# Loading weights from another queue, starting two groups side by side, and splitting a deferred product in the last group

## Chip, cores and metric

One core of one Trainium2 chip. All times are device microseconds of that core. The kernel before takes 3486.24 us (median of 3 runs, 3485.54 to 3486.57). Engine names: PE is TensorE, DVE is VectorE, ACT is ScalarE, POOL is GpSimd, SP is SyncE.

## The reference, cut to what matters

Two graph layers, one after the other, on 64 graphs of 256 nodes and 256 features, all in 32-bit floats. The adjacency matrices hold 0 and 1.

```python
x    # (64, 256, 256) float32
adj  # (64, 256, 256) int32, 0 or 1

def gat(h, adj, W, a):                       # twice, W1/a1 and W2/a2
    Wh = h @ W
    e  = leaky_relu(Wh @ a[:F] + swap(Wh @ a[F:]), 0.2)
    return softmax(where(adj > 0, e, -9e15), axis=1) @ Wh

# layer 0
h = layernorm(x + gat(gat(x)), g_ln1, b_ln1)
x = layernorm(h + relu(h @ w_ff1 + b_ff1) @ w_ff2 + b_ff2, g_ln2, b_ln2)
# layer 1: 8 heads of 32; one value matrix per kind of edge (adj == r)
attn = softmax(q @ k.T / sqrt(32))
out  = sum over r of (attn * (adj == r)) @ (x @ Wv[r] + bv[r])
x = layernorm(x + out @ Wo + bo, g1, beta1)
out = layernorm(x + gelu(x @ W1 + b1) @ W2 + b2, g2, beta2)
```

## The kernel before

It takes the graphs in 32 groups of two. A "turn" interleaves the second layer of group `y_`, the feed-forward of the first layer of group `x_ = y_ + 1`, and the graph attention of group `z = y_ + 2`. The order of TensorE's products is the program's order (`manual_schedule`). The parts that matter here, with cuts marked `# ...`:

```python
def load(u):
    xs = io.tile([P, T, F], F32, tag="xs", name=f"xs{u}")          # 2 buffers
    nc.sync.dma_start(xs, x[G * u:G * (u + 1)]...)
    af = io.tile([P, T, N], F32, tag="af", name=f"af{u}", bufs=1)  # 1 buffer
    nc.gpsimd.dma_start(af, adj[G * u:G * (u + 1)]...)
loaded = {0: load(0)}
# ...
def weight(w, name):                       # column() and row() likewise
    t = const.tile([P, w.shape[0] // P, w.shape[1]], F32, name=name)
    nc.scalar.dma_start(t, w.rearrange("(c p) f -> p c f", p=P))
# ... combined graph weights gwe, then some 30 loads on the scalar queue
nc.vector.tensor_tensor(wv[:, :, 1, :], wv[:, :, 1, :], wv[:, :, 0, :], ALU.subtract)
nc.vector.tensor_tensor(rbv[:, F:], rbv[:, F:], rbv[:, :F], ALU.subtract)
# ...
nc.gpsimd.tensor_add(rb1, rb1, rbf2)
nc.gpsimd.tensor_add(rb2, rb2, rbo)
nc.gpsimd.tensor_add(rb3, rb3, rbt2)

def projected(u, hT):                      # xpp, copied out by ACT into xp
    # ...
        nc.scalar.copy(xp[:, t, :], ps[:, :WX])

def normed(u, l, y):
    for t in range(T):
        nc.vector.bn_stats(st[:, t, :], y[:, t, :])
        nc.vector.bn_aggr(mv[:, t, :], st[:, t, :])
    nc.vector.tensor_scalar(ve, mv[:, :, 1], EPS, None, op0=ALU.add)
    nc.gpsimd.tensor_tensor(rs, ve, mhalf, ALU.pow)
    # ...
    for t in range(T):
        nc.vector.tensor_scalar(y[:, t, :], y[:, t, :], mv[:, t, 0:1], rs[:, t:t + 1],
                                op0=ALU.subtract, op1=ALU.mult)

def affine(u, l, xn, g, b):
    r = work.tile([P, T, F], F32, tag="res", name=f"res{u}_{l}", bufs=3)
    nc.gpsimd.tensor_mul(r, xn, g[:, None, :].to_broadcast([P, T, F]))
    nc.gpsimd.tensor_add(r, r, b[:, None, :].to_broadcast([P, T, F]))

def second_sums(x_):                       # ygp: second attention, residual, norm
    # ...
    d["y"] = normed(x_, 0, y)
    d["res"] = affine(x_, 0, d["y"], rg1, rb1)

def turn(y_, x_, z):
    if z + 1 < NG:
        g[z + 1]["xs"], g[z + 1]["af"] = load(z + 1)
    if have(y_): hT = to_features(Y["y"], f"h2T{y_}", lg2, lb2)
    if have(x_): second_sums(x_)
    if have(y_): q, k_ = queries_keys(y_, hT)
    # ... interleaved work of y_, x_ and z
    if have(y_):
        yf = hidden_out(y_, 1, h1, w2, res)          # the last product of a group
        yn = normed(y_, 3, yf)
        res = affine(y_, 3, yn, rg4, rb4)
        nc.sync.dma_start(out[G * y_:G * (y_ + 1)]..., res)

with tc.manual_schedule(engines={mybir.EngineType.PE}):
    for u in range(-2, NG):
        turn(u, u + 1, u + 2)
```

Names of products in the profile: `xpp` projection, `rows` transposed scores, `hpp` first attention sums, `ygp` second attention sums, `h1p` and `yfp` the two feed-forward products, `h1T`, `h2T`, `h3T` transposed and scaled activations, `qp`, `kp`, `vp` queries, keys, values. A number after a name is the group.

## Time and profile before

| | before |
|---|---|
| median of 3 runs | 3486.24 us |
| span of the profiled run | 3486.0 us |
| PE busy | 97% |
| one steady turn (from qp of group 1 to qp of group 2) | 105.79 us |
| fill: start of qp of group 0 | 128.11 us |
| drain: from the end of the last full turn's h1p (3380.15) to the end | 105.85 us |

The prediction shows the lines for this, and takes the start of `qp` of group 0 as the mark for the fill. One more part of the page matters, the DMA queues: the scalar queue (q10) moved 7.76 MB, nearly all of it weights, and the sync queue (q1) 33.56 MB.

### The profile page before, as it was taken

The page shows a single profiled execution, that of the slowest core. Times are in us where ns is not written, and L with a number is a line of the kernel's source. Part 1 is how long each engine was busy: PE and PEld are TensorE (multiplying, and loading weights), DVE is VectorE, ACT ScalarE, POOL GpSimd, SP SyncE. Part 2 cuts the span into 40 slices and gives each one's busy share as a digit, 9 for nine tenths or more (in the row PEclk, how much of TensorE's full clock was granted, in tenths as well). Part 3 has the DMA queues.
Part 4 walks back from the last instruction along what each step waited for, and adds up shares of the span by engine and source line. Part 5 has one row for each costly group of instructions (what it writes and reads, how often), then busy time and mean ns, then how long its engine had stood idle before and what let it go on. Part 6 is the DMA issues. An engine that isn't in the chain of part 4 may idle for free.

```text
span 3486.0 us, 45212 instructions
## 1 busy us (share of the span) xinstructions
PE 3368.1 (97%) x18970; PEld 2201.8 (63%) x18970; DVE 1688.8 (48%) x3479; ACT 1080.4 (31%) x1920; POOL 984.6 (28%) x844
## 2 busy tenths in 40 slices
PE   5899999999999999999999999999999999999997
PEld 3566666666665666665666666666656665656664
DVE  2545455445454444554454554454544445544544
ACT  1323333323323323333333333233233233333322
POOL 1233232332222332322332323322223323223312
PEclk7999999999999999999999999999999999999998
DMA  4000000000000000000000000000000000000000
GB/s 119 19 13 19 7 19 19 13 19 10 16 19 19 13 19 7 19 19 19 13 19 7 19 19 13 19 12 14 19 19 13 19 7 19 19 19 7 7 1 14
DMA packets 62465, 61.04 MB, mean 18 GB/s; under 512 B 7216, under 2 KB 61616, under 8 KB 62256
## 3 DMA queue, kind: packets, MB, share of 16 engines
q1 hardware_dynamic: 33792, 33.56, 3.0%
q0 software_dynamic: 16896, 16.78, 2.1%
q10 hardware_dynamic: 11568, 7.76, 0.8%
q8 instruction: 151, 2.47, 0.3%
q14 instruction: 58, 0.48, 0.0%
HBM read 41.31 MB, written 16.78 MB: 17 GB/s over the span
## 4 chain that ended last, share of the span: by engine, by line
PE 86%; POOL 6%; DVE 6%; issue 1%; ACTq 1%; DMA 0%; ACT 0%; POOLq 0%; DVEq 0%
PE h1p L655 26%; PE yfp L617 25%; PE vp L686 6%; PE po L722 6%; PE sp L702 4%; PE zo L722 4%; PE hpp L606 3%; PE yop L617 3%; PE xpp L568 3%; POOL res L644 2%; POOL res L645 2%; POOL rs L633 2%; DVE yf L637 1%; DVE h2T L544 1%; PE rows L578 1%
## 5 line engine op out<-in xcount | busy, mean ns | idle before, releaser
L655 PE MATMUL h1p<-h1T,wf 128*128 128x512 f32 x1024 | 458.1, 600 | 0.1
L710 DVE TENSOR_TENSOR ea<-e,aT 128x1024 f32<-128x1024 f32 x256 | 317.9, 1283 | 272.7 <-ACT e L708 272.7
L655 PE MATMUL h1p<-h3T,w 128*128 128x512 f32 x1024 | 446.7, 594 | 1.4 <-DVE h3T L544 1.4
L617 PE MATMUL yfp<-wf,h 128*128 128x256 f32 x2048 | 447.3, 379 | 0.0
L617 PE MATMUL yfp<-w,h 128*128 128x256 f32 x2048 | 447.3, 379 | 0.0
L617 PEld LDWEIGHTS yfp<-w,h 128*128 128x128 f32 x2048 | 386.8, 190 | 52.2 <-issue 1.0
L617 PEld LDWEIGHTS yfp<-wf,h 128*128 128x128 f32 x2048 | 386.7, 190 | 51.3
L708 ACT ACTIVATE e<-sp 128x512 f32<-128x512 f32 x512 | 264.3, 603 | 444.9 <-PE sp L702 444.9
L655 PEld LDWEIGHTS h1p<-h3T,w 128*128 128x128 f32 x1024 | 195.0, 191 | 234.4 <-issue 229.5
L729 POOL TENSOR_TENSOR low<-low,rz 128x512 f32<-128x512 f32 x64 | 81.2, 1269 | 917.2 <-DVE rz L728 917.2
L655 PEld LDWEIGHTS h1p<-h1T,wf 128*128 128x128 f32 x1024 | 190.1, 190 | 236.9 <-issue 218.2
L587 DVE SCALAR_TENSOR_TENSOR s<-s 128x512 f32<-128x512 f32 x128 | 90.2, 706 | 443.3 <-ACT s L584 442.0
L645 POOL TENSOR_TENSOR res<-res,rb 128x1024 f32<-128x1024 f32 x128 | 301.3, 2354 | 10.0
L620 DVE TENSOR_TENSOR yf<-yfp,res 128x512 f32<-128x512 f32 x128 | 88.5, 692 | 424.6 <-PE yfp L617 423.4
L633 POOL TENSOR_TENSOR rs<-ve,mhalf 128x4 f32<-128x4 f32 x128 | 130.7, 1021 | 457.9 <-DVE ve L632 457.9
L657 ACT ACTIVATE h<-h1p,b 128x512 f32<-128x512 f32 x256 | 175.9, 687 | 251.1 <-PE h1p L655 249.8
L728 DVE RECIPROCAL rz<-zo 128x512 f32<-128x512 f32 x64 | 214.7, 3354 | 67.8 <-PE zo L722 67.8
L657 ACT ACTIVATE h<-h1p,bf 128x512 f32<-128x512 f32 x256 | 177.1, 692 | 216.0 <-PE h1p L655 216.0
L686 PE MATMUL vp<-wv,h2T 128*128 128x512 f32 x512 | 225.0, 592 | 0.0
L676 ACT ACTIVATE q<-qp,bq 128x512 f32<-128x512 f32 x64 | 44.0, 688 | 530.8 <-PE qp L674 530.8
L608 ACT COPY hp<-hpp 128x258 f32<-128x258 f32 x128 | 48.0, 375 | 442.0 <-PE hpp L606 442.0
L644 POOL TENSOR_TENSOR res<-yf,rg 128x1024 f32<-128x1024 f32 x64 | 150.8, 2356 | 95.8 <-DVE yf L637 94.3
(485 smaller groups left out, 4343.4 us busy)
## 6 DMA issues: line engine op xcount, KB each, us to landing
xs<-in_x_dram SPq DMA_DIRECT2D x32, 512.0 KB, 3.8
af<-in_adj_dram POOLq DMA_DIRECT2D x32, 512.0 KB, 4.5
out_dram<-res SPq DMA_DIRECT2D x32, 512.0 KB, 2.9
wf<-in_L_gnn_w_ff_dram ACTq DMA_DIRECT2D x2, 1024.0 KB, 11.4
w<-in_L_gnn_W_dram ACTq DMA_DIRECT2D x2, 1024.0 KB, 9.5
wv<-in_L_gnn_Wv_dram ACTq DMA_DIRECT2D x2, 256.0 KB, 4.5
gw<-in_L_gnn_W_dram ACTq DMA_DIRECT2D x1, 256.0 KB, 4.5
gw2e<-in_L_gnn_W_dram ACTq DMA_DIRECT2D x1, 256.0 KB, 6.9
```

The lines of the kernel that those rows point to most:

```text
L617: nc.tensor.matmul(ps[:, i * F:(i + 1) * F], lhs(t, k), rhs(b, k), start=(k == 0), stop=(k == n - 1))
L633: nc.gpsimd.tensor_tensor(rs, ve, mhalf, ALU.pow)
L644: nc.gpsimd.tensor_mul(r, xn, g[:, None, :].to_broadcast([P, T, F]))
L645: nc.gpsimd.tensor_add(r, r, b[:, None, :].to_broadcast([P, T, F]))
L655: nc.tensor.matmul(ps, wi[:, k, f * P:(f + 1) * P], hT[:, k, :], start=(k == 0), stop=(k == KB - 1))
L657: nc.scalar.activation(h1[:, f, :], ps, func, bias=bi[:, f:f + 1])
L686: nc.tensor.matmul(ps, hT[:, k, t * P:(t + 1) * P], wvf[:, k, :], start=(k == 0), stop=(k == KB - 1))
L702: nc.tensor.matmul(ps[a][:, j * N:(j + 1) * N], k_[hp, m, j0:j0 + P], q[hp, m, b * N:(b + 1) * N], start=True, stop=True)
L708: nc.scalar.activation(e[:, a, :], ps[a], AF.Exp, scale=isd)
L710: nc.vector.tensor_tensor(ea[:, a:a + 2, :], e[:, a:a + 2, :], ab[:, None, :].to_broadcast([P, 2, NB * N]), ALU.mult)
L722: nc.tensor.matmul(to[hp, m * N:(m + 1) * N], lhs(m * HPB + a, j), rhs[:, a, j * N:(j + 1) * N], start=(n < 2 and j == 0), stop=(n != 1 an ...
L728: nc.vector.reciprocal(rz, zo)
```

## The change

It has three parts. **Part 1**: nearly all weights are loaded from the sync queue, so that ACT's own queue is free for arithmetic early. **Part 2**: the empty turns -2 and -1 are replaced by a fill that runs groups 0 and 1 side by side, so that the softmax waits of one are covered by products of the other. **Part 3**: the last product of group 30 is cut into four pieces that are put into the waits of the last turn, and the output of both last groups is normalised and stored by graph. The diff, cut to its core:

```diff
-    loaded = {0: load(0)}
 def weight(w, name):
-        nc.scalar.dma_start(t, w...)
+        nc.sync.dma_start(t, w...)
 # row() the same; column() too, apart from the attention vectors a1, a2; w2e and wv too
 gwe = gat_weights()
+    for u in range(2):
+        g[u]["xs"], g[u]["af"] = load(u)
 # normed() and affine() get an argument for some of the blocks
+    def out_pieces(u, h1, res):            # a generator: hidden_out in four pieces,
+        for b in range(G):                 # 16 matmuls each
+            for i in range(NB):
+                # ... 16 matmuls into one bank
+                if i == NB - 1:
+                    # add, normed, affine and store of graph b alone
+                yield
 def turn(y_, x_, z):
+        if y_ == 0: g[z]["xs"], g[z]["af"] = load(z)
         if have(y_): hT = to_features(Y["y"], f"h2T{y_}", lg2, lb2)
+        piece()
-        if have(x_):
+        if have(x_) and y_ > 0:
             second_sums(x_)
 # piece() also before apply_(0), after apply_(3) and after affine(y_, 2, ...)
-        if have(y_):
+        if y_ == NG - 2:
+            left.append((out_pieces(y_, h1, res)))
+        elif y_ == NG - 1:
+            for _ in out_pieces(y_, h1, res): pass
+        else:
             yf = hidden_out(y_, 1, h1, w2, res)
-        for u in range(-2, NG):
+        for stage in (early, project, first_scores): stage(0)
+        for stage in (early, project, first_scores): stage(1)
+        for stage in (first_sums, second_scores): stage(0)
+        for stage in (first_sums, second_scores): stage(1)
+        second_sums(0)
+        hT = to_features(g[0]["y"], "h1T0", lg1, lb1)
+        h1 = hidden(0, 0, hT, wf1, bf1, AF.Relu, range(FB))
+        yf = hidden_out(0, 0, h1, wf2, g[0]["res"])
+        second_sums(1)
+        g[0]["y"] = normed(0, 1, yf)
+        g[0]["res"] = affine(0, 1, g[0]["y"], rg2, rb2)
+        for u in range(NG):
             turn(u, u + 1, u + 2)
```

More of the change, by code (lines that the diff above doesn't have):

```diff
@@ L455, in weight, with column @@
         t = const.tile([P, w.shape[0] // P, w.shape[1]], F32, name=name)
-        nc.scalar.dma_start(t, w.rearrange("(c p) f -> p c f", p=P))
+        nc.sync.dma_start(t, w.rearrange("(c p) f -> p c f", p=P))
         return t
-    def column(v, name):
+    def column(v, name, queue=nc.sync):
         n = v.shape[0] // P
         t = const.tile([P, n], F32, name=name)
-        nc.scalar.dma_start(t, v.rearrange("(c p) -> p c", p=P))
+        queue.dma_start(t, v.rearrange("(c p) -> p c", p=P))
         return t
@@ L467, in row @@
         t = const.tile([P, n], F32, name=name)
-        nc.scalar.dma_start(t, bass.AP(tensor=v.tensor, offset=v.offset, ap=[[0, P], [1, n]]))
+        nc.sync.dma_start(t, bass.AP(tensor=v.tensor, offset=v.offset, ap=[[0, P], [1, n]]))
         return t
@@ L475, in gat_weights @@
         w2e = work.tile([P, KB, WX], F32, tag="wh", name="gw2e")
-        nc.scalar.dma_start(w2e[:, :, :F], g_W2.rearrange("(c p) f -> p c f", p=P))
-        a1 = column(g_a1.rearrange("f o -> (f o)"), "ga1")
-        a2 = column(g_a2.rearrange("f o -> (f o)"), "ga2")
+        nc.sync.dma_start(w2e[:, :, :F], g_W2.rearrange("(c p) f -> p c f", p=P))
+        a1 = column(g_a1.rearrange("f o -> (f o)"), "ga1", nc.scalar)
+        a2 = column(g_a2.rearrange("f o -> (f o)"), "ga2", nc.scalar)
         def transposed(w, name):
@@ L506, in narrow_path @@
     gwe = gat_weights()
+    g = {u: {} for u in range(NG)}
+    for u in range(2):
+        g[u]["xs"], g[u]["af"] = load(u)
     wf1, wf2 = weight(g_wf1, "wf1"), weight(g_wf2, "wf2")
@@ L518, in narrow_path @@
     for r in range(2):
-        nc.scalar.dma_start(wv[:, :, r, :], t_Wv[r].rearrange("(c p) f -> p c f", p=P))
+        nc.sync.dma_start(wv[:, :, r, :], t_Wv[r].rearrange("(c p) f -> p c f", p=P))
     rbv = row(t_bv[0:2].rearrange("r f -> (r f)"), "rbv")
@@ L621, in add_blocks, with normed @@
                                 res[:, bt, :].rearrange("p t f -> p (t f)"), ALU.add)
-    def normed(u, l, y):
-        st = work.tile([P, T, 6], F32, tag="st", name=f"st{u}_{l}")
-        mv = work.tile([P, T, 2], F32, tag="mv", name=f"mv{u}_{l}")
-        ve = work.tile([P, T], F32, tag="ve", name=f"ve{u}_{l}")
-        rs = work.tile([P, T], F32, tag="rs", name=f"rs{u}_{l}")
-        for t in range(T):
+    def normed(u, l, y, blocks=range(T)):
+        n, t0 = f"{u}_{l}_{blocks[0]}", blocks[0]
+        bt = slice(t0, t0 + len(blocks))
+        st = work.tile([P, T, 6], F32, tag="st", name=f"st{n}")
+        mv = work.tile([P, T, 2], F32, tag="mv", name=f"mv{n}")
+        ve = work.tile([P, T], F32, tag="ve", name=f"ve{n}")
+        rs = work.tile([P, T], F32, tag="rs", name=f"rs{n}")
+        for t in blocks:
             nc.vector.bn_stats(st[:, t, :], y[:, t, :])
             nc.vector.bn_aggr(mv[:, t, :], st[:, t, :])
-        nc.vector.tensor_scalar(ve, mv[:, :, 1], EPS, None, op0=ALU.add)
-        nc.gpsimd.tensor_tensor(rs, ve, mhalf, ALU.pow)
+        nc.vector.tensor_scalar(ve[:, bt], mv[:, bt, 1], EPS, None, op0=ALU.add)
+        nc.gpsimd.tensor_tensor(rs[:, bt], ve[:, bt], mhalf[:, bt], ALU.pow)
         if l == 3:
-            nc.gpsimd.tensor_add(high, high, mv[:, :, 0])
-        for t in range(T):
+            nc.gpsimd.tensor_add(high[:, bt], high[:, bt], mv[:, bt, 0])
+        for t in blocks:
             nc.vector.tensor_scalar(y[:, t, :], y[:, t, :], mv[:, t, 0:1], rs[:, t:t + 1],
@@ L639, in normed, with affine @@
         return y
-    def affine(u, l, xn, g, b):
-        r = work.tile([P, T, F], F32, tag="res", name=f"res{u}_{l}", bufs=3)
-        nc.gpsimd.tensor_mul(r, xn, g[:, None, :].to_broadcast([P, T, F]))
-        nc.gpsimd.tensor_add(r, r, b[:, None, :].to_broadcast([P, T, F]))
+    def affine(u, l, xn, g, b, r=None):
+        if r is None:
+            r = work.tile([P, T, F], F32, tag="res", name=f"res{u}_{l}", bufs=3)
+        nc.gpsimd.tensor_mul(r, xn, g[:, None, :].to_broadcast(list(r.shape)))
+        nc.gpsimd.tensor_add(r, r, b[:, None, :].to_broadcast(list(r.shape)))
         return r
@@ L732, in divided @@
                                 rz.rearrange("p (m n) -> p m n", m=KB), ALU.mult)
-    g = {u: {} for u in range(NG)}
     def early(z):
@@ L766, in second_sums, with piece @@
         d["res"] = affine(x_, 0, d["y"], rg1, rb1)
+    left = []
+    def out_pieces(u, h1, res):
+        y = work.tile([P, T, F], F32, tag="y", name=f"yf{u}_1")
+        r = work.tile([P, T, F], F32, tag="res", name=f"res{u}_3", bufs=3)
+        for b in range(G):
+            ps = bank(f"yfp1_{u}_{b}")
+            for i in range(NB):
+                t = b * NB + i
+                for k in range(FB):
+                    nc.tensor.matmul(ps[:, i * F:(i + 1) * F], h1[:, k, t * P:(t + 1) * P], w2[:, k, :],
+                                     start=(k == 0), stop=(k == FB - 1))
+                if i == NB - 1:
+                    bt = slice(b * NB, (b + 1) * NB)
+                    nc.vector.tensor_tensor(y[:, bt, :].rearrange("p t f -> p (t f)"), ps,
+                                            res[:, bt, :].rearrange("p t f -> p (t f)"), ALU.add)
+                    normed(u, 3, y, range(b * NB, (b + 1) * NB))
+                    affine(u, 3, y[:, bt, :], rg4, rb4, r[:, bt, :])
+                    nc.sync.dma_start(out[G * u + b].rearrange("(c p) f -> p c f", p=P), r[:, bt, :])
+                yield
+    def piece():
+        if left:
+            next(left[0], None)
     def turn(y_, x_, z):
@@ L770, in have @@
             return 0 <= u < NG
+        if y_ == 0:
+            g[z]["xs"], g[z]["af"] = load(z)
         if z + 1 < NG:
@@ L801, in turn @@
             e[1] = weighted(y_, *quads[1], q, k_, aT)
+            piece()
             apply_(0)
@@ L812, in turn @@
             apply_(3)
+            piece()
         if have(y_):
@@ L828, in turn @@
             res = affine(y_, 2, yn, rg3, rb3)
+            piece()
         if have(x_):
@@ L840, in turn @@
             second_scores(z)
-        if have(y_):
+        if y_ == NG - 2:
+            left.append((out_pieces(y_, h1, res)))
+        elif y_ == NG - 1:
+            for _ in out_pieces(y_, h1, res):
+                pass
+        else:
             yf = hidden_out(y_, 1, h1, w2, res)
@@ L845, in turn, with first_sums @@
             nc.sync.dma_start(out[G * y_:G * (y_ + 1)].rearrange("b (c p) f -> p (b c) f", p=P), res)
-    g[0]["xs"], g[0]["af"] = loaded.pop(0)
+    def first_sums(z):
+        g[z]["hp"] = gat_first(z, g[z]["s"], g[z]["xp"])
     with tc.manual_schedule(engines={mybir.EngineType.PE}):
-        for u in range(-2, NG):
+        for stage in (early, project, first_scores):
+            stage(0)
+        for stage in (early, project, first_scores):
+            stage(1)
+        for stage in (first_sums, second_scores):
+            stage(0)
+        for stage in (first_sums, second_scores):
+            stage(1)
+        second_sums(0)
[6 more added lines that the diff above has]
+        for u in range(NG):
             turn(u, u + 1, u + 2)
```

## The prediction

> **What bounds the kernel now.** I began with the page's first two parts, to see which engine sets the time and where it is idle.
>
> ```profile
> PE 3368.1 (97%) x18970; PEld 2201.8 (63%) x18970; DVE 1688.8 (48%) x3479; ACT 1080.4 (31%) x1920; POOL 984.6 (28%) x844
> PE   5899999999999999999999999999999999999997
> PEclk7999999999999999999999999999999999999998
> DMA  4000000000000000000000000000000000000000
> ```
>
> TensorE is busy for 97% of the span; the gaps are in the first two slices (87 us each) and the last one. In between nothing is to be had: the matmul timeline shows the same product (the queries of groups 1 and 2) one period apart, 337.54 - 231.75 = 105.79 us, with a wait of only 1.4 us in it. 32 x 105.79 = 3385, so about 100 us of the 3486 are fill and drain, and the change touches only these. Next the fill, in the timeline of TensorE (start, us, what, idle before it):
>
> ```profile
> 20.06 3.93 PE L568 MATMUL xpp<-gwe,xT 128*128 128x260 f32 x16 [1.06 <-DVE xT L542]
> 41.82 1.31 PE L578 MATMUL rows<-ident,xp 128*128 128x128 f32 x4 [17.83 <-ACT xp L570]
> 48.01 5.56 PE L606 MATMUL hpp<-xp,s 128*128 128x258 f32 x16 [4.88 <-POOL xp L596]
> 59.24 6.74 PE L617 MATMUL ygp<-hp,s 128*128 128x256 f32 x16 [4.88 <-POOL hp L596]
> ...
> 122.38 5.90 PE L617 MATMUL ygp<-hp,s 128*128 128x256 f32 x16 [8.00 <-POOL hp L596]
> 128.11 3.60 PE L674 MATMUL qp<-h2T,wq 128*128 128x512 f32 x8
> ```
>
> Group 0 runs alone through a chain of softmax waits, and group 1 has another 8 us wait before its second sums. From qp of group 0, at 128.1 us, the kernel is in its steady rhythm. So the fill's worth is how much earlier that one product starts. The longest wait, 17.8 us on ACT, is explained by ACT's own waits (waiter, releaser, us, times, longest):
>
> ```profile
> ACT L557 <- DMA lb<-in_L_gnn_beta_dram: 39.1, 1, 39.1
> ```
>
> ACT did no arithmetic for 39.1 us because all its weight loads stand ahead in its queue; its timeline has single issues of 3.9, 4.35 and 5.23 us. The drain is the last group alone:
>
> ```profile
> 3380.15 13.98 PE L617 MATMUL yfp<-w,h 128*128 128x256 f32 x64
> 3393.96 1.04 PE L540 MATMUL h2T31p<-ident,yf 128*128 128x128 f32 x8
> 3424.18 1.94 PE L722 MATMUL zo<-e,ones 128*32 128x256 f32 x16 [3.02 <-DVE rz L728]
> 3439.36 1.65 PE L540 MATMUL h3T31p<-ident,yo 128*128 128x128 f32 x8 [3.63 <-DVE yo L637]
> 3456.84 13.98 PE L617 MATMUL yfp<-w,h 128*128 128x256 f32 x64
> ```
>
> Its waits are short (3.02, 3.63, some of 0.3 to 0.6), and after the last product the chain that ended last has VectorE and GpSimd from 3470.85 to 3480.1 and then a 512 KB store.
>
> **What the Trainium skill says.** "DMA: Bandwidth & Descriptors", section "Issuing engines are not separate DMA queues": loads from every queue share the same 16 DMA engines, so another queue saves only issuing time. The trace agrees: 0 to 20 us ran at DMA share 0.89 and 227 GB/s, 20 to 40 at 0.90 and 247. Moving the loads frees ACT but doesn't make the weights land sooner. "TensorE: Matmul & The Clock Gate", section "Part 1: The HAM clock gate": after an idle window of about 3.4 us the clock halves, and it returns after as much sustained work. The trace agrees: granted clock 0.50 from 30 to 42 us, and hpp took 5.56 us there against 3.64 warm. "SBUF — State Buffer", section "Who interferes with whom": VectorE and GpSimd share one pair of ports, held for a whole instruction ("it's an exclusive lock"). The trace fits: two softmax steps on VectorE took 4.58 us beside GpSimd's affine at 114.7 us, against 1.42 alone at 96.2.
>
> **Part 1, weights from the sync queue.** Only gw1 and the two vectors of attention coefficients stay on ACT. ACT is free from some 4 us on, so its copies of xp follow the product at 20.06, and rows of group 0 starts near 24.3 instead of 41.8 (last copy 0.4 us after the product ends): 17.5 us off group 0's chain.
>
> **Part 2, groups 0 and 1 side by side.** The order on TensorE is fixed: early, project and first scores of 0, the same of 1, then first sums and second scores of each, second sums of 0, both feed-forward products of 0, second sums of 1. Everything behind group 1's adjacency waits for its landing; call that time L. From L, by warm durations of the trace: two transposes 1.7, wait for VectorE's copy 1.1, xpp 3.7, copy and rows 0.8; hpp0 3.6. Two buffers of tag wh hold xp0 and xp1, so hp0's four copies (0.38 each) can only follow the last hpp0 matmul: with rows 2.1. hpp1 3.6 and again 2.1, ygp0 3.6. That is 22.3. The second softmax of 0 (5.8 us from rows to sums before) fits beside hpp1 and its copies. Then the normalisation wait 3.6, h1T0 with its evacuation 2.0, h1p 13.7, yfp 13.8, ygp1 3.5 (it covers most of yf's normalisation, about 4 us), h2T0 and evacuation 2.0: L + 60.9. For slow clock after the remaining idle stretches I add 4 (before, hpp, ygp and h1p lost 1.9, 3.1 and 2.1): qp at L + 65.
>
> L itself: there is one adjacency buffer, freed by VectorE at 19.4 us before. If the load goes out at once it issues at 20.5 and lands after 8.2 us (the median of the three early ones): L = 29, **qp at 94**. But GpSimd issues that load, and before it stood behind two additions that wait for weights (rb, at 24.88 and 26.08; the load went out at 26.75). Now another 0.5 MB of x lies ahead of those weights, 2.2 us at 230 GB/s; the load goes out near 29 and lands at 37: **qp at 102**. A similar thing: GpSimd's third addition waited for the last weights until 42.66 before, ahead of the scaling that releases hpp0; if it stands so again, hpp0 starts at 43.5 and qp also comes near 102. I take the middle, **98**, thus 128.1 - 98 = **30 us** gained.
>
> **Part 3, the deferred product in pieces.** The product of group 30, 13.8 us, leaves its place and comes back as four pieces of 16 matmuls, 13.98 / 4 = 3.5 us each, in the last turn. The gain is only the waits that they cover. Piece one, behind h2T31: covers 0.63 + 0.31. Piece two, before the first applied scores: shifts everything behind it equally, so the 3.02 wait for the reciprocal stays. Piece three: covers the 0.64 wait and little more, 0.9. Piece four: covers the 3.63. Sum 5.4. Against it: a PSUM bank is held between pieces one and two, so the second score product finds one bank less (0.9), and the first half's normalisation and GpSimd's affine come near the ea products on VectorE (about 1). Net **3.3 us**.
>
> The last group's output by halves: after the last matmul the chain was add 0.7, statistics 1.0, pow 1.2 with its neighbours, subtract 1.38, affine 2.35 + 2.34, some 9.3 us. With half of it left: subtract 0.8, affine 1.2 + 1.2, about 6.2. That is 3.1, and the halved store saves about 0.3: **3.4 us**.
>
> The fetch of two groups in turn 0 moves no time: both are needed some 40 us later or more. Sum: 3486.2 - 30.1 - 3.3 - 3.4 = **3449.4 us**.
>
> **Rivals.** (a) *A landing takes the place of the issue wait.* If in-order VectorE and GpSimd stand behind weights (VectorE waited 9.9 us for wv until 30.5 before, GpSimd 15.1 for the last ones), freeing ACT buys less, qp moves to 102 or, with the attention coefficients also delayed by competing loads, to 107: 3453 to 3459. For it: DMA share 0.9 until 40 us. Against it: the order on these engines may change with the program's order. (b) *All overlaps well.* TensorE's own work from the end of the combined weights (16.8) to qp is 26 for the two attentions, 28.4 for the feed-forward, 0.9 for h2T0: qp at 72 is the floor. With L = 27 and a warm clock qp is near 88: 3440. The floor itself would give 3423, still only 1.8%. (c) *Contention in the drain:* pieces put GpSimd's affine beside ea on VectorE, each up to 2.4 us late, and the reciprocal wait grows: part 3 nets nothing, 3453. (d) *Steady turns change.* Their program is the same; nothing speaks for it.
>
> **Range and chances.** Fill 22 to 40 us, drain 3 to 10; both ends together are rare, so 3438 to 3464 should hold 8 times in 10. Over 2% faster would need 70 us of the 100 that are not steady, more than the floor of (b) allows with a good drain; over 2% slower would need a steady turn 2.2 us longer. So within 2%: 0.965, faster 0.02, slower 0.015.
>
> **What would show it.** Right: ACT's first copy before 20 us; rows of group 0 near 24; qp of group 0 at 94 to 102, and the period still 105.8; the 3.63 wait of h3T31 gone, a wait for the reciprocal of at least 3 us still there; 6 us instead of 9 from the last add to the store. Wrong: rows of group 0 after 30 us (the coefficients' loads were slowed), the period off by over 0.2 us, or a new wait for a PSUM bank between the pieces.

## The result, and the profile after

The changed kernel takes 3466.40 us (median of 6 runs, 3464.54 to 3467.91); the kernel before took 3485.89 us beside it (6 runs, 3483.94 to 3486.57). The ratio is 0.9944, 95% interval 0.9932 to 0.9957: within 2%, as predicted, but a gain of 19.5 us instead of 36.8, 2.4 us outside the predicted range. A ratio in this document is the ratio of one kernel's runs to those of the kernel before, run beside it; it is not quite the ratio of the medians quoted. All outputs are right.

From the page of the changed kernel, the parts that the prediction showed of the kernel before:

```profile
PE 3367.2 (97%) x18970; PEld 2201.4 (64%) x18970; DVE 1690.6 (49%) x3481; ACT 1079.6 (31%) x1920; POOL 985.7 (28%) x852
...
PE   7899999999999999999999999999999999999997
...
PEclk9999999999999999999999999999999999999999
```

PE's first slice (87 us) went from 0.5 to 0.7, and the second stayed at 0.8: the gain is in the first. The granted clock is now 0.9 or more in every slice, where the first had 0.7 and the last 0.8. The page's queues show that the weights moved: 0.27 MB are left on q10, and q1 has 41.05 MB.

The fill in TensorE's timeline (start, us, engine, line, operation, names, count, and idle before it with its releaser):

```profile
26.35 0.95 PE L579 MATMUL rows<-ident,xp 128*128 128x128 f32 x4
31.50 1.94 PE L556 MATMUL aTp<-ident,af 128*128 128x128 f32 x8 [4.20 <-DMA af<-in_adj_dram]
...
37.60 5.59 PE L569 MATMUL xpp<-gwe,xT 128*128 128x260 f32 x16 [2.58 <-DVE xT L543]
...
43.81 3.66 PE L607 MATMUL hpp<-xp,s 128*128 128x258 f32 x16
...
63.02 2.30 PE L541 MATMUL h1T0p<-ident,yg 128*128 128x128 f32 x8 [5.22 <-DVE yg L640]
...
94.75 3.62 PE L618 MATMUL ygp<-hp,s 128*128 128x256 f32 x16
109.34 2.30 PE L541 MATMUL h2T0p<-ident,yf 128*128 128x128 f32 x8 [10.98 <-DVE yf L640]
111.69 4.46 PE L678 MATMUL qp<-h2T,wq 128*128 128x512 f32 x8
```

Part 1 did on TensorE's queue what it should: `rows` of group 0 starts at 26.35 instead of 41.82. The adjacency of group 1 came at 31.50, inside the predicted 29 to 37. From there `qp` was to follow 65 us later; it followed 80.2 us later, at **111.69 instead of the predicted 98**. The largest new wait, 10.98 us, stands directly ahead of the mark: `h2T0` waits for the normalised `yf`. The prediction had put nothing there.

What VectorE and GpSimd did in those 11 us, from the timeline of all engines:

```profile
100.86 1.02 POOL L636 TENSOR_TENSOR rs<-ve,mhalf 128x4 f32<-128x4 f32 x1 [32.09 <-DVE ve L635]
101.92 1.38 DVE L640 TENSOR_SCALAR yg<-yg,mv,rs 128x256 f32<-128x256 f32 x4 [0.68 <-POOL rs L636]
...
103.38 2.34 POOL L648 TENSOR_TENSOR res<-yg,rg 128x1024 f32<-128x1024 f32 x1 [1.50 <-DVE yg L640]
103.43 2.32 DVE L635 TENSOR_SCALAR ve<-mv 128x4 f32<-128x4 f32 x1
105.83 1.01 POOL L636 TENSOR_TENSOR rs<-ve,mhalf 128x4 f32<-128x4 f32 x1
...
106.87 3.39 DVE L640 TENSOR_SCALAR yf<-yf,mv,rs 128x256 f32<-128x256 f32 x4 [1.12 <-POOL rs L636]
```

`ygp` of group 1 ended at 98.4. From then on group 1 (`yg`) and group 0 (`yf`) compete. Their statistics alternate on VectorE, and then **group 1 goes first at every step**: its power at 100.86, its subtraction at 101.92, its affine on GpSimd at 103.38. Only then comes `ve` of group 0, a 128x4 addition, at 103.43. It took 2.32 us beside GpSimd's multiplication of 2.34 us; group 1's own `ve` at 100.63 took 0.15. The subtraction of `yf` took 3.39 us beside GpSimd's addition, that of `yg` 1.38. In the program, `second_sums(1)` stands ahead of `normed(0, 1, yf)`, and these engines took the two groups in that order.

The drain (the lines answer to those that the prediction shows):

```profile
3366.01 1.04 PE L541 MATMUL h2T31p<-ident,yf 128*128 128x128 f32 x8
...
3403.43 1.72 PE L726 MATMUL zo<-e,ones 128*32 128x256 f32 x16 [4.09 <-DVE rz L732]
...
3421.24 1.64 PE L541 MATMUL h3T31p<-ident,yo 128*128 128x128 f32 x8 [0.18 <-DVE yo L640]
...
3437.85 13.98 PE L781 MATMUL yfp<-w,h 128*128 128x256 f32 x64
```

The wait of `h3T31` fell from 3.63 to 0.18 us, and the wait for the reciprocal stayed, both as predicted; it also grew from 3.02 to 4.09, of which rival (c) had warned. From 3366.01 to the end it is 98.3 us, against 105.85 us before: 7.6 us gained, 6.7 predicted. From the start of `h2T31` to that of the last product it went from 3456.84 - 3393.96 = 62.88 us with the deferred product ahead of it (13.81 us more, 76.69) to 3437.85 - 3366.01 = 71.84 us with it inside: 4.9 us. The rest, 2.7 us, is the shorter tail from the start of the last product (29.2 us before, 26.5 now).

The account of the spans, 3486.0 - 3464.3 = 21.7 us: `qp` of group 0 is 16.4 us earlier, but `qp` of a late group (1924.42 before, 1910.43 after) only 14.0. The 2.4 us were lost in turns 0 and 1: the first `qp` itself took 4.46 us instead of 3.60, and `vp` of turn 1 took 8.56 us instead of 7.03 at a granted clock of 0.66. Behind these the turns have their old length, 105.8. 14.0 + 7.6 = 21.6, so nothing is missing. The medians differ by 2.2 us less than the spans, because the profiled run of the kernel before lay 1.8 us above its median (3487.73 against 3485.89) and that of the changed kernel 0.4 us below (3466.02 against 3466.40). So a sum taken from two traces can miss the medians by about 2 us.

### The profile page after: what moved, and what is told of

Read it like the earlier page. It is cut to its first block, busy times and chain, and to the rows that moved or that the text cites. A ratio compares the mean times of both kernels' runs of the same rounds, so it can differ in the third digit from the quotient of the medians.

```text
span 3464.3 us, 45233 instructions
## 1 busy us (share of the span) xinstructions
PE 3367.2 (97%) x18970; PEld 2201.4 (64%) x18970; DVE 1690.6 (49%) x3481; ACT 1079.6 (31%) x1920; POOL 985.7 (28%) x852
## 3 DMA queue, kind: packets, MB, share of 16 engines
q1 hardware_dynamic: 44064, 41.05, 3.8%
q8 instruction: 151, 2.47, 0.3%
## 4 chain that ended last, share of the span: by engine, by line
PE 86%; POOL 6%; DVE 6%; issue 1%; DMA 1%; ACT 0%; POOLq 0%; DVEq 0%; ACTq 0%
PE h1p L659 26%; PE yfp L618 25%; PE vp L690 6%; PE po L726 6%; PE sp L706 4%; PE zo L726 4%; PE yop L618 3%; PE hpp L607 3%; PE xpp L569 3%; POOL res L648 2%; POOL res L649 2%; POOL rs L636 2%; DVE yf L640 1%; DVE h2T L545 1%; PE rows L579 1%
## 5 line engine op out<-in xcount | busy, mean ns | idle before, releaser
L618 PE MATMUL yfp<-w,h 128*128 128x256 f32 x1920 | 419.4, 379 | 0.0
L618 PEld LDWEIGHTS yfp<-w,h 128*128 128x128 f32 x1920 | 362.5, 190 | 48.0
L649 POOL TENSOR_TENSOR res<-res,rb 128x1024 f32<-128x1024 f32 (+1 forms) x130 | 302.0, 2323 | 10.1
L636 POOL TENSOR_TENSOR rs<-ve,mhalf 128x4 f32<-128x4 f32 (+1 forms) x130 | 131.4, 1011 | 468.7 <-DVE ve L635 468.5
L648 POOL TENSOR_TENSOR res<-yf,rg 128x1024 f32<-128x1024 f32 (+1 forms) x66 | 150.8, 2285 | 95.9 <-DVE yf L640 95.1
```

Of the source, the lines that this page charges most:

```text
L618: nc.tensor.matmul(ps[:, i * F:(i + 1) * F], lhs(t, k), rhs(b, k), start=(k == 0), stop=(k == n - 1))
L636: nc.gpsimd.tensor_tensor(rs[:, bt], ve[:, bt], mhalf[:, bt], ALU.pow)
L648: nc.gpsimd.tensor_mul(r, xn, g[:, None, :].to_broadcast(list(r.shape)))
L649: nc.gpsimd.tensor_add(r, r, b[:, None, :].to_broadcast(list(r.shape)))
```

## The experiments

**Theory**: the fill lost what the prediction expected because group 0's normalisation stands behind group 1's on VectorE and GpSimd. **Rivals**: (R1) the wait is contention with GpSimd's affine alone, whatever the order; (R2) the fill is bound by landing weights and adjacency, and the order changes nothing; (R3) part 1 brings the whole gain, and running the groups side by side was never worth anything.

### norm_first: group 0's normalisation ahead of group 1's sums

```diff
         yf = hidden_out(0, 0, h1, wf2, g[0]["res"])
-        second_sums(1)
         g[0]["y"] = normed(0, 1, yf)
         g[0]["res"] = affine(0, 1, g[0]["y"], rg2, rb2)
+        second_sums(1)
```

TensorE's order is the same, since the moved lines give it nothing to do.

> The changed kernel with two lines moved: group 0's second normalisation and affine stand ahead of group 1's second sums in the program. TensorE's order is the same. Theory (the 10.98 us wait of h2T0 comes from the order of VectorE and GpSimd, where group 1's normalisation and affine stand ahead of group 0's): h2T0 waits at most 1 us after ygp1, qp of group 0 starts near 101 instead of 111.7, and the kernel takes 3455 to 3457 us, ratio to before about 0.991. Rival A (the wait is the normalisation's own latency behind the last yfp matmul): the wait stays over 7 us and the time over 3462. Rival B (the gain is taken back, because group 1's normalisation is now late for h1T1): h2T0 is early, but a new wait of over 4 us stands before h1T1.

Measured: 3455.76 us (4 runs, 3452.98 to 3457.65), before 3486.60, ratio 0.9909 (0.9894 to 0.9924). Its timeline of all engines:

```profile
98.61 1.02 POOL L636 TENSOR_TENSOR rs<-ve,mhalf 128x4 f32<-128x4 f32 x1 [28.53 <-DVE ve L635]
99.66 1.38 DVE L640 TENSOR_SCALAR yf<-yf,mv,rs 128x256 f32<-128x256 f32 x4 [0.54 <-POOL rs L636]
...
100.13 1.73 PE L541 MATMUL h2T0p<-ident,yf 128*128 128x128 f32 x8
...
103.92 2.67 PE L678 MATMUL qp<-h2T,wq 128*128 128x512 f32 x4 [2.06 <-DVE h2T L545]
```

The power follows at 98.61 instead of 105.83, `yf` is normalised while `ygp` of group 1 runs, and `h2T0` starts at 100.13 with no idle time of TensorE worth a note (0.08 us after `ygp` of group 1 ends). The kernel gains 10.6 us on the changed one by medians and 8.4 by the spans of the two profiled runs (3464.3 and 3455.9); the profiled run here was the slowest of its four. `qp` starts at 103.92, not near 101 as expected: one new wait, 2.06 us for `h2T`, shows the same thing once more on a small scale, since the first half of `h2T`'s scaling starts only at 103.09, behind group 1's addition and statistics on VectorE. Rival B's wait before `h1T1` did not appear. So the step failed by its order: the 3.5 us of `ygp` do cover the normalisation once it may go first.

### affine_late: only GpSimd's affine of group 1 moved back

```diff
         d["y"] = normed(x_, 0, y)
-        d["res"] = affine(x_, 0, d["y"], rg1, rb1)
+        if x_ != 1:
+            d["res"] = affine(x_, 0, d["y"], rg1, rb1)
 # ... and in the fill, after affine(0, 1, ...):
+        g[1]["res"] = affine(1, 0, g[1]["y"], rg1, rb1)
```

> The changed kernel with only group 1's affine on GpSimd moved behind group 0's normalisation in the program; VectorE's order is as in the changed kernel. It divides the 10.98 us wait. Theory: GpSimd's affine multiply of group 1 (2.34 us), which delays the power of group 0 and holds up a VectorE step for 2.32 us, is some 4 us of it: h2T0 waits about 7 us, time 3462 us. If VectorE's order alone made the wait: still 10 to 11 us, 3466. If GpSimd alone made it: under 2 us, 3456.

Measured: 3462.99 us (5 runs, 3458.29 to 3466.41), before 3486.60, ratio 0.9931 (0.9917 to 0.9944). The timeline of all engines in the same stretch:

```profile
102.89 0.17 DVE L635 TENSOR_SCALAR ve<-mv 128x4 f32<-128x4 f32 x1
103.13 1.01 POOL L636 TENSOR_TENSOR rs<-ve,mhalf 128x4 f32<-128x4 f32 x1 [1.79 <-DVE ve L635]
104.18 1.38 DVE L640 TENSOR_SCALAR yf<-yf,mv,rs 128x256 f32<-128x256 f32 x4 [1.12 <-POOL rs L636]
...
104.65 2.30 PE L541 MATMUL h2T0p<-ident,yf 128*128 128x128 f32 x8 [6.82 <-DVE yf L640]
```

Without GpSimd's multiplication beside it the same 128x4 addition took 0.17 us, and the wait fell from 10.98 to 6.82 us: 4.2 us of it came from the affine on GpSimd, the other 6.8 us from group 1's sums, statistics, power and subtraction ahead in order. The 4.2 us have two halves. From the end of `ygp` to the power it is 2.2 us less; there the addition was slowed, but group 0's power also stood behind the multiplication in GpSimd's own order (103.38 + 2.34 = 105.72, power at 105.83), and no run separates the two. From the start of the subtraction of `yf` to `h2T0` it is 2.0 us less (0.47 instead of 2.47), and in this half only the contention is left. So R1 holds for 2.0 us and perhaps for 4.2, not for the whole wait. By medians it gained 3.4 us, and the intervals of the two kernels' ratios overlap, so the trace says more here than the times.

### queue_only: the kernel before with part 1 alone

```diff
-        nc.scalar.dma_start(t, w...)
+        nc.sync.dma_start(t, w...)
 # weight, row, column, w2e and wv as in the change; nothing else
```

> The kernel before with part 1 alone (weights from the sync queue). The prediction says that rows of group 0 starts near 24 to 26 us instead of 41.8. Theory: most of these 17 us come through only as far as VectorE and GpSimd, which stand in order behind late weights (wv and the value bias landed near 31 to 35 us), so that the first sums of group 0 start near 36 instead of 48: qp of group 0 at 115 to 118 and 3474 us in all. Rival (ACT's block was all that held the chain): first sums near 32, 3470. Rival (weights landing hold it to the end): 3480 or more.

Measured: 3473.73 us (5 runs, 3472.53 to 3474.78), before 3486.60, ratio 0.9962 (0.9949 to 0.9976): 12.9 us. `qp` of group 0 starts at 115.62, 12.5 us earlier. Its timeline of all engines shows why it isn't the 17.5 us by which `rows` was to move:

```profile
25.30 0.95 PE L578 MATMUL rows<-ident,xp 128*128 128x128 f32 x4
...
28.98 0.69 DVE L521 TENSOR_TENSOR wv<-wv 128x512 f32<-128x512 f32 x1 [6.90 <-DMA wv<-in_L_gnn_Wv_dram]
...
31.20 0.42 DVE L522 TENSOR_TENSOR rbv<-rbv 128x256 f32<-128x256 f32 x1 [1.53 <-DMA rbv<-in_L_gnn_bv_dram]
...
35.48 5.58 PE L606 MATMUL hpp<-xp,s 128*128 128x258 f32 x16 [9.22 <-POOL xp L596]
```

`rows` starts 16.5 us earlier than before, yet `hpp` only 12.5 (48.01 before). ACT had the scores ready by 27.9 (it started them at 26.30 and took 1.57), but VectorE waited for `wv` until 28.98 and for `rbv` until 31.20, for two subtractions whose results are not used before turn 0. Only then does it take the scores. That is the prediction's rival (a), a landing in place of the issue wait, and it costs about 4 us here.

### queue_back: the changed kernel without part 1

```diff
-        nc.sync.dma_start(t, w...)
+        nc.scalar.dma_start(t, w...)
 # weight, row, column, w2e and wv back on the scalar queue
```

> The changed kernel with part 1 undone (weights from ACT's queue again), so parts 2 and 3 alone. Theory: ACT starts near 40 us, rows of group 0 near 42, group 1's stages follow behind, first sums of group 0 start near 49 instead of 43.8 in the changed kernel; about 6 us are lost: 3472 us. The 11 us wait of h2T0 stays. Rival (the queue is worth all of the gain in the fill): 3480 or more. Rival (side by side hides the block whole, because the landing of the second adjacency held the changed kernel just as long): 3467.

Measured: 3476.66 us (5 runs, 3476.29 to 3478.25), before 3486.60, ratio 0.9974 (0.9960 to 0.9987). `rows` of group 0 waits 17.50 us for ACT and starts at 41.49, and `qp` at 121.96. Part 1 is thus worth 10.3 us with the other parts there and 12.9 without. The expectation of 3472 us was missed: `hpp` of group 0 starts at 54.22, not near 49, because all of group 1's early stages stand ahead of it on TensorE and now follow `rows` at 41.49. `h2T0` waits 10.97 us here as well: that wait doesn't come from when the weights land, against R2.

### no_side: the changed kernel without part 2

```diff
+    loaded = {0: load(0)}
-    for u in range(2):
-        g[u]["xs"], g[u]["af"] = load(u)
+    g[0]["xs"], g[0]["af"] = loaded.pop(0)
 # ... the fill list taken out
-        for u in range(NG):
+        for u in range(-2, NG):
             turn(u, u + 1, u + 2)
```

> The changed kernel with part 2 undone: groups 0 and 1 in the order of the kernel before, weights from the sync queue and the pieces kept. Theory: with the weights from the sync queue alone qp of group 0 came at 115.6 us, in the changed kernel at 111.7, and the colder clock there gave 2 us back, so part 2 is worth about 2 us as it stands: 3466 to 3468 us, the same as the changed kernel within 3 us. Rival (part 2 carries the gain in the fill, as the prediction's sum has it, some 10 us beyond part 1): 3476.

Measured: 3466.25 us (5 runs, 3464.45 to 3467.23), before 3485.89, ratio 0.9943 (0.9930 to 0.9957). That is the changed kernel's time, 3466.40: **as written, part 2 is worth nothing that these runs can show.** TensorE's timeline:

```profile
109.14 5.64 PE L618 MATMUL ygp<-hp,s 128*128 128x256 f32 x16 [8.00 <-POOL hp L597]
114.62 3.60 PE L678 MATMUL qp<-h2T,wq 128*128 128x512 f32 x8
```

`qp` starts at 114.62, 2.9 us later than in the changed kernel, but takes its full-clock 3.60 us, and the turns behind it lose nothing: 13.5 us at `qp` and 7.6 of part 3 make 21.1, and the span is 21.4 us shorter than before. Running the groups side by side took away the waits of 4.88 (twice) and 8.00 us that the prediction showed, and put the 10.98 us wait and the clock loss in their place. R3 holds for the change as it stands and fails with norm_first: there part 2 is worth 3466.25 - 3455.76 = 10.5 us, if the two are taken as comparable (they ran beside different runs of the kernel before, 3485.89 and 3486.60).

### no_pieces: the changed kernel without part 3

```diff
-        if y_ == NG - 2:
-            left.append((out_pieces(y_, h1, res)))
-        elif y_ == NG - 1:
-            for _ in out_pieces(y_, h1, res):
-                pass
-        else:
+        if True:
             yf = hidden_out(y_, 1, h1, w2, res)
```

> The changed kernel with part 3 undone: group 30's product whole in its place, group 31's output in one. From the traces the drain (from the end of h1p of group 30 to the end) went from 105.85 to 98.3 us, so it costs 7.5 us: 3474 us. By the prediction 6.7: 3473. Rival (the drain's gain is the last group's output by halves alone): 3470.

Measured: 3474.95 us (5 runs, 3474.30 to 3475.27), before 3485.89, ratio 0.9969 (0.9955 to 0.9983). Part 3 is worth 8.5 us by medians and 7.6 by the changed kernel's trace; the prediction had 6.7. The waits that the pieces cover are back: 0.63 and 0.31 us on `qp` of group 31, 3.63 on `h3T31`; and its `h1p` began at a lower granted clock after that wait, 0.61 from 3429 to 3434 (15.77 us in all, in the changed kernel 14.6 from its first to its last matmul). The prediction had not counted that.

### norm_early: norm_first and a buffer of its own for group 1's adjacency

```diff
-        af = io.tile([P, T, N], F32, tag="af", name=f"af{u}", bufs=1)
+        if u == 1:
+            af = work.tile([P, T, N], F32, tag="ea", name=f"af{u}")
+        else:
+            af = io.tile([P, T, N], F32, tag="af", name=f"af{u}", bufs=1)
 # and norm_first's edit; the tag "ea" is not used before turn 0
```

> norm_first with group 1's adjacency in a buffer of its own (one that the first attention uses later), so that its load needs not wait for group 0's. Tests whether its landing, at 31.5 us in the changed kernel, is what sets the fill. Theory: only in part, since VectorE then stands behind the late weights (wv and its bias, landed by 35 us) before it can copy xT of group 1: hpp of group 0 starts at 41 instead of 45, 3451 to 3452 us. Rival (the landing alone sets it): hpp at 36, 3446. Rival (nothing, the clock and the order hold it): 3455.

Measured: 3455.18 us (5 runs, 3454.64 to 3456.73), before 3485.89, ratio 0.9914 (0.9901 to 0.9928): norm_first's time. The wait for the adjacency is gone, and one of 7.93 us takes its place in TensorE's timeline (the transposes of group 1 end near 29.0):

```profile
36.91 5.72 PE L572 MATMUL xpp<-gwe,xT 128*128 128x260 f32 x16 [7.93 <-DVE xT L546]
```

`xpp` of group 1 waits for VectorE's copy of `xT1`, and VectorE stands behind the two subtractions that wait for `wv` and `rbv`. The earlier adjacency was worth nothing by itself that the times show, and the expected 3451 to 3452 us was missed.

### load_order: rows, wv and rbv loaded ahead of the feed-forward weights

```diff
 # norm_early, and in the order of the loads:
+    rg1, rb1, rg2, rb2 = row(...) ...
+    rbf2, rbo, rbt2 = row(...) ...
+    rg3, rb3, rg4, rb4 = row(...) ...
+    wv = ...; rbv = row(...)
     wf1, wf2 = weight(g_wf1, "wf1"), weight(g_wf2, "wf2")
```

> norm_early with the loads in the order of need: the rows, wv and its bias ahead of the feed-forward weights, so that VectorE's and GpSimd's early additions wait for nothing late. Theory (those in-order waits are what remains): aT of group 1 follows rows of group 0 without a wait, hpp of group 0 starts at 35 to 37, h1p near 57, 3445 to 3447 us. Rival (feed-forward weights now land too late, or the coefficients' small loads are slowed further): h1p waits for wf by over 2 us or gwap starts after 15 us, 3450 or more.

Measured: 3455.39 us (5 runs, 3453.56 to 3457.35), before 3485.89, ratio 0.9912 (0.9898 to 0.9925): the same again. `wv` came earlier, and in the order of VectorE's work the subtraction then stood between the two copies of the combined weights, ahead of group 0's first product. From the timeline of all engines:

```profile
23.79 0.69 DVE L526 TENSOR_TENSOR wv<-wv 128x512 f32<-128x512 f32 x1 [6.73 <-DMA wv<-in_L_gnn_Wv_dram]
...
27.41 6.53 PE L572 MATMUL xpp<-gwe,xT 128*128 128x260 f32 x16 [6.76 <-DVE xT L546]
```

VectorE waited 6.73 us for `wv` and TensorE 6.76 us for what came behind it. The wait had moved from group 1's `xpp` to group 0's. The expected 3445 to 3447 us was missed, and not by the rival's signs: `gwap` started at 12.82 and `h1p` waited for no weight.

### wv_tied: the two subtractions made to follow group 0's first feed-forward input

```diff
-    nc.vector.tensor_tensor(wv[:, :, 1, :], wv[:, :, 1, :], wv[:, :, 0, :], ALU.subtract)
-    nc.vector.tensor_tensor(rbv[:, F:], rbv[:, F:], rbv[:, :F], ALU.subtract)
 # norm_early, and after hT = to_features(g[0]["y"], "h1T0", lg1, lb1):
+        nc.vector.tensor_scalar(one, hT[:, 0, 0:1], 0.0, 1.0, op0=ALU.mult, op1=ALU.add)
+        nc.vector.scalar_tensor_tensor(wv[:, :, 1, :], wv[:, :, 1, :], one, wv[:, :, 0, :],
+                                       op0=ALU.mult, op1=ALU.subtract)
+        # the same for rbv
```

The factor `one` is 1.0 made out of `h1T0`, so the subtractions cannot be ordered ahead of it.

> norm_early with VectorE's two subtractions of value weights tied, by a factor of one computed from h1T of group 0, to a point behind both softmaxes, so that they cannot stand ahead of them. In norm_early the wait for xT of group 1 (7.9 us) took the place of the wait for the adjacency. Theory (that wait is VectorE standing in order behind the late wv and its bias): xpp of group 1 starts near 31 instead of 36.9, hpp of group 0 at 35 to 36 instead of 43.3, 3446 to 3448 us. Rival (some other step of VectorE or ACT holds xT, as ACT's queue or the softmax of group 0): xpp still after 35, 3453 to 3455.

Measured: 3455.15 us (4 runs, 3453.64 to 3456.02), before 3487.44, ratio 0.9908 (0.9892 to 0.9925): the same a third time. Its timeline of all engines shows the next one in the row:

```profile
44.90 0.95 POOL L534 TENSOR_TENSOR rb<-rb,rbt 128x256 f32<-128x256 f32 x1 [11.21 <-DMA rb<-in_L_gnn_beta_dram]
...
46.52 5.70 PE L609 MATMUL hpp<-xp,s 128*128 128x258 f32 x16 [5.08 <-POOL xp L599]
```

`xpp` of group 1 starts at 30.05 (36.91 in norm_early), and `hpp` of group 0 at 36.11 (43.26), but GpSimd waits 11.21 us for the last row of weights, for the addition `rb3 + rbt2` that nothing needs before turn 0's second layer, and the scaling of `xp` that releases `hpp` of group 1 stands behind it: 5.08 us. So the expected 3446 to 3448 us was missed although `xpp` and `hpp` came where the theory had them. It is the prediction's "if it stands so again", one group later.

### all_five: that row loaded early, and the coefficients first

```diff
 # wv_tied, and
+        a2 = column(g_a2..., "ga2", nc.scalar)     # first on the scalar queue
+        a1 = column(g_a1..., "ga1", nc.scalar)
-        nc.scalar.dma_start(w1s, ...)
+        nc.sync.dma_start(w1s, ...)
-    rbf2, rbo, rbt2 = row(g_bf2, "rbf2"), row(t_bo, "rbo"), row(t_b2, "rbt2")
+    rbf2, rbo, rbt2, rb3 = row(g_bf2, "rbf2"), row(t_bo, "rbo"), row(t_b2, "rbt2"), row(t_be1, "rb3")
```

> wv_tied with the two attention coefficients' loads ahead of everything on ACT's queue, gw1 on the sync queue and one row load (beta1) earlier. In the changed kernel gwap waited 6.6 us for a coefficient until 13.4. If their place in the queue sets their landing: gwap near 10 to 11, the whole fill 2 to 3 us earlier, 3444 to 3446 us. Rival (they are slow because big loads of the other queues share the engines): gwap still near 13, no gain over wv_tied.

Measured: **3443.83 us** (4 runs, 3442.48 to 3444.33), before 3487.44, ratio 0.9875 (0.9858 to 0.9891). It beats the kernel before by 43.6 us and the changed kernel by 22.6 (by medians). TensorE's timeline:

```profile
7.54 1.87 PE L494 MATMUL gwap<-ga,gw2t 128*128 128x2 f32 x8 [1.10 <-DVE gw2t L487]
...
31.49 3.66 PE L609 MATMUL hpp<-xp,s 128*128 128x258 f32 x16
...
90.24 5.40 PE L680 MATMUL qp<-h2T,wq 128*128 128x512 f32 x8 [2.05 <-DVE h2T L547]
```

The product with the attention coefficients starts at 7.54 instead of 13.42, because the two small loads stand first in their queue; no wait for a weight is left between it and `qp`, which starts at 90.24. This run joins two edits, the early row and the early coefficients; which brought how much of the 11.3 us isn't separated by a run. Against wv_tied, over which the 11.3 us are counted, `gwap` starts 4.0 us earlier (11.57 to 7.54; it varied from 11.57 to 13.42 among the kernels with part 1 and the old order of the coefficients). By the two traces these 4.0 us, the missing wait of 5.08 us and `hpp` of group 1 behind it, back from 5.70 to 3.66 us, make up the 11.2 us at `qp` (101.42 to 90.24).

## Why the prediction was wrong, point by point

- **The bound**: right. TensorE's turns kept 105.8 us from turn 2 on, and only fill and drain changed.
- **Part 1**: right in its mechanism and slightly too large. `rows` of group 0 was to start near 24.3 and started at 26.35, because the coefficients landed later (`gwap` at 13.42 instead of 11.29). ACT's first copy came at 19.83, before 20 us as forecast.
- **L, the landing of group 1's adjacency**: 31.5, inside the two cases of 29 and 37. GpSimd issued the load at 22.23, ahead of its two additions, as in the first case; it took 9.3 us from there to the transpose that it released.
- **Part 2, from L to `qp`**: the step that failed is "ygp1 3.5 (it covers most of yf's normalisation, about 4 us)". It assumed that VectorE and GpSimd would take `yf` of group 0 first. In the program, `normed(0, 1, yf)` stands after `second_sums(1)`, and they took group 1 first, at 10.98 us of waiting. norm_first shows that the order was the cause: with it turned round, the product covers the normalisation. affine_late shows that 4.2 us of the wait came from group 1's affine on GpSimd, at least 2.0 of them by the contention for which the prediction had cited the skill, and which its sum had allowed for in the drain alone.
- **The allowance for the clock**, 4 us: too small. Transposes 1.8, `xpp` 1.7, `h1p` 1.9, and `h1T` and `h2T` 0.35 each over their warm durations make 6.1 us.
- **Two waits of the same kind as the failed step**: `xT1` waited 2.58 instead of 1.1 us, because VectorE did softmax steps of group 0 and the two weight subtractions ahead of the copy (34.63 to 36.86), and `yg` of group 0 waited 5.22 instead of 3.6, with softmax steps of group 1 between (55.23 to 58.54). This is read from VectorE's order in the trace; no run tests it.
- The terms add up: against the predicted 98, where L was 33 in the middle, L gave -1.5, the `yf` wait +11.0, the clock +2.1 beyond the allowance, the wait for `xT1` +1.5, the wait for `yg` +1.6, the copies with `rows` -1.1 and small terms +0.2. That is 13.8, and 111.7 - 98 is 13.7.
- **"qp's start is the fill's worth"**: 2.4 us short. The first `qp` and `vp` of turn 1 ran at a lower clock, so 16.4 us at the mark were 14.0 in the steady turns.
- **Part 3**: right and slightly too small, 7.6 instead of 6.7: the pieces 4.9 instead of 3.3, the halved output 2.7 instead of 3.4. No wait for a PSUM bank over 0.26 us appeared between the pieces.
- **Rivals**: (a) was there. In the changed kernel the adjacency's landing hid it; in queue_only it cost about 4 us, and once norm_first and the new buffer were in, it was the bound three times running. (b) was off by the order above: all_five, with that and the late weights mended, has `qp` at 90.24, near the 88 that (b) named as possible. (c) came true in part: the wait for the reciprocal grew by 1.07 us, but part 3 still gained 7.6. (d) did not occur beyond turn 1.
- **Two sums of the prediction don't close**: for the pieces, 5.4 - 0.9 - 1 is 3.5, not 3.3, and for (c), part 3 netting nothing would give 3456, not 3453, which is the pieces alone netting nothing. Neither matters here.
- **The range** was too narrow for a fill whose sum had some fifteen terms and one untested assumption on order: 13.7 us came from that sum.

Open: how the 11.3 us of all_five divide between its two edits, which share of the first 2.2 us in affine_late is contention, and why the low-clock stretches vary by 1 us or so from one kernel to the next (the same 16 `xpp` matmuls of group 1 took from 5.27 us in queue_back to 6.75 in affine_late).

## What to carry to other kernels

When two streams of work are interleaved by hand, the order must be read on every engine, not only on the one that is scheduled: a product covers a wait only if the engine that ends the wait comes to it first. In a fill, look for work on in-order engines that waits for data needed much later, and move both the work and its load; where several such waits stand one behind the other, removing one shows no gain until the last is gone, as norm_early, load_order and wv_tied showed with 3455 us each. Test such edits together as well as alone.

## What the Trainium skill lacked or had wrong

- "DMA: Bandwidth & Descriptors", section "Issuing engines are not separate DMA queues", says that issuing from several engines saves only the sequencer's time for the issue, "usually small relative to the DMA itself". Here it was not small: single issues of 4, 1 and 1 KB vectors held ACT for 3.91, 4.35 and 5.23 us (the last with 9.1 us from issue to landing), ACT's first instruction waited 39.1 us, and moving the loads was worth 12.9 us alone (queue_only). The page doesn't say that a queue of issues holds up its engine's arithmetic.
- "SBUF — State Buffer", section "Who interferes with whom": agreed, and the size was surprising: an instruction on very few elements can be held as long as the other engine's large one. A VectorE addition on 128x4 elements took 2.32 us beside a GpSimd multiplication of 2.34 us, and 0.17 us without it (affine_late).
- No page has a size for what the strict order of VectorE's and GpSimd's instructions costs when an early one waits for late data and holds up unrelated later ones: 6.90 us on VectorE in queue_only, 11.21 us on GpSimd in wv_tied.
- No page says how much a place in the queue matters for tiny loads: behind one or two 256 KB loads the attention vectors (2 KB each) held their product until 11.29 to 13.42 us in all the other kernels; first in their queue, they no longer held it, and it started at 7.54 us (all_five).
